# A planner in the kernel fixes the order of TensorE, VectorE and ScalarE

## The chip, the cores and the metric

The kernel runs on one core of a Trainium2 chip. Its engines are TensorE (PE in the profile, with PEld for its weight loads), VectorE (DVE), ScalarE (ACT), GpSimd (POOL, which also issues DMAs here) and SyncE (SP, which only issues DMAs). Each takes its own queue of instructions in order, and waits for the others by semaphores. The metric is the device time of one execution, in microseconds (us); lower is better.

## What is computed

Two layers on x of shape 4 x 1024 x 256, all in float32. Each has a mixer `s` and a gate `g` on the normalized x, and adds `s * silu(g)`. The parts that matter, cut from the reference:

```python
x = L0_attn_x
xn = _layernorm(x)
s = _L0_attn_ref(xn, ...)            # linear attention on cos/sin features, then an MLP
g = _silu(_L0_ffn_ref(xn, ...))      # r * (relu(k)**2 @ W_v), tokens mixed with the one before
x = x + s * g
xn = _layernorm(x)
s = _L1_attn_ref(xn, ...)            # Mamba: convolution, then the scan below
g = _silu(_L1_ffn_ref(xn, ...))      # two of eight experts for each token, one after the other
x = x + s * g

# _L1_attn_ref: token after token, 512 channels x 16 states
dA = exp(dt_t[:, :, None] * A)
h = h * dA + (dt_t * u_t)[:, :, None] * B_t[:, None, :]
y = einsum('bcs,bs->bc', h, C_t)
```

## The kernel before

**Tiling.** Tokens are cut into 8 blocks of 512. Layer 0 works on two blocks (`s`) of each of 4 sequences (`b`). `before_attention` normalizes a block (`normalize`, L195 to L214: statistics L202 and L203 on DVE, a power on POOL at L205 and L212, the product at L218), transposes it and makes queries, keys and values (the bias of the values is added at L273). `cycle` (L1190) takes one group of features at a time: `project_keys` or `project_queries` (matmuls fk at L425, fq at L436), `fractions` (L458 to L461: the rounding on ACT at L460 or DVE at L458, the fraction on DVE at L461), `sines` on ACT, and `use_keys` or `use_queries` (kv at L497, pa at L528). `after_attention` does the rest of layer 0 for a block: output projection po (x at L306), MLP ph and py (x at L350), gate g (L388), and writes the block to DRAM; the router's logits `gate` come at L411.

**Scans.** In layer 1 a block's 512 channels are two units of 256, and each unit has 16 scan steps, one for each state: 8 x 2 x 16 = 256 steps. For a step `decay` (L636) loads B and C (`bcs`, L642, by SP, three buffers) and makes `da` on ACT (L192, four buffers); `scan_step` (L690) multiplies on DVE (L710), scans (L713 or L719), and multiplies by C (L728); PE transposes and adds into `y` (L731). `prepare_block` (L549) makes `u` for a block: its load `xt` (L553), matmul pi, the convolution on DVE (L572), SiLU, and matmul pd. `prepare_unit` makes `dt` (L610 to L616) and `dtu` (L628). At the end of a unit `ys` (L756) multiplies by the gate, and `project_block` copies the projection `s` (L781) and stores it in `branch`.

**Experts.** `experts` (L844) ranks the tokens on DVE (L889 to L958), giving `slot` (L945); POOL scatters all tokens into `slots` in 32 indirect DMAs (L968). Then 23 tiles of 256 tokens run twice: `fetch` (weights `we` L982, rows `xs` L987), `hidden_layer` (pxs L1001, xst L1005, ph and ht L1017), `output_layer` (po, es L1030, xs L1034 and L1039) and two scatters. The last normalization is at L1085 to L1105.

**What sets the order.** The Python code calls these parts as generators: `Stream.step` takes the next piece of a stream, and `cycle` deals out pieces of the four streams (attention before, attention after, scan side work, experts) between two scan steps. That is only the order in which instructions are written down. The framework's own scheduler then orders each engine's instructions by this priority, by data and by buffers, with a cost model of its own; it also puts in the semaphores. One chain was fixed by hand: `in_turn` (L171) ties each special function of ACT, and each load of an activation table, to the one before, so that tables are not loaded back and forth:

```python
def in_turn(i):
    if last[0] is not None:
        tc.add_manual_dep(i.ins, last[0].ins.name, ...)   # NoSync: order alone
    last[0] = i
```

Of the kernel before, what the change touches and what calls it, by code (L numbers as in the profile page):

```python
# [2 lines left out]

# [15 lines left out]
PSUM = bass.MemoryType.PSUM  # L19
DRAM = bass.MemoryType.DRAM  # L20

P = 128
# [33 lines left out]
for _n, _w in _COLS:  # L56
    COL[_n] = NCOL
    NCOL += _w


@with_exitstack
def kernel(
# [3 lines left out]
    nc = tc.nc  # L66
# [22 lines left out]
    def tokens(ap):  # L89
        return ap.rearrange("(t p) d -> p t d", p=P)  # L90
# [75 lines left out]

    now, last = [None], [None]

    def in_turn(i):  # L171
        if last[0] is not None:
            tc.add_manual_dep(
                i.ins, last[0].ins.name,
                mybir.DependencyInfo(
                    mybir.DependencyClass.NoSync, mybir.DependencyReason.SCHED_ONLY
                ),
            )
        last[0] = i

    def functions(which):
        if now[0] != which:
            in_turn(
                nc.scalar.preload_act_table_set(  # L184
                    {"E": "natural_log_exp_and_others", "S": "silu_and_others"}[which]
                )
            )
            now[0] = which

    def special(out, in_, func, **kw):  # L190
        functions("E" if func in (AF.Exp, AF.Ln) else "S")
        in_turn(nc.scalar.activation(out, in_, func, **kw))  # L192
# [278 lines left out]
    turns = [0]  # L471
# [8 lines left out]
    kv, kvp, pa, at = {}, {}, {}, {}  # L480
# [207 lines left out]
    sums, late = {}, []  # L688
# [76 lines left out]
    def branch_halves(j):  # L765

        for i in range(NT // 2):
            ps = bank(f"ps_{j}{i}").rearrange("p (u d) -> p u d", u=2)
            for w in range(2):
                sl = slice((2 * i + w) * P, (2 * i + w + 1) * P)  # L770
                accumulate(
                    ps[:, w, :],
                    [(halves[j, c // UNIT][:, c % UNIT, sl], wout_s[:, c, :]) for c in range(NDI)],
                )
            yield ps
# [30 lines left out]
    ready, projected, left = [], set(), []  # L806
# [20 lines left out]
    for k, t in enumerate(slots):  # L827
        a = t[:NPAD, :].rearrange("(a p) d -> p a d", p=P)
# [281 lines left out]
    def finish(j, xm, s, xn):  # L1110

        for i, ps in enumerate(branch_halves(j)):
            two = slice(2 * i, 2 * i + 2)
            nc.vector.tensor_tensor(s[:, two, :], ps, xn[:, two, :], ALU.mult)
            nc.vector.tensor_tensor(s[:, two, :], s[:, two, :], xm[:, two, :], ALU.add)
            first = j * TB + 2 * i * P
            nc.sync.dma_start(out=tokens(out[first : first + 2 * P, :]), in_=s[:, two, :])
# [142 lines left out]
    turn_half(NBLK - 1, 1)  # L1260
    for one in left:
        finish(*one)


def _layout(inputs):
# [68 lines left out]
```

## Time and profile before

| | us |
|---|---|
| three runs | 2339.23, 2330.81, 2336.70 (median 2336.7) |
| the profiled execution | 2339.8 |
| its span, first to last instruction | 2338.1 |

The profile is of one execution. Its first part gives the busy time of each engine, its second the same in 40 slices of 58 us. The costliest groups, with line, engine, operation, tiles and shapes, count, busy us, mean ns, and the idle time before them with what ended it:

| group | count | busy us | mean ns |
|---|---|---|---|
| L192 ACT `da`, 128x512 | 512 | 334.4 | 716 |
| L731 PE `y`, 128x128 | 2048 | 314.1 | 302 |
| L728 DVE `da`, 128x1024 | 256 | 310.8 | 1215 |
| L713 DVE scan, 128x1024 | 128 | 290.7 | 2281 |
| L710 DVE `h`, 128x1024 | 240 | 288.6 | 1212 |
| L719 DVE scan, 128x512 | 224 | 276.2 | 1267 |
| L184 ACT table load | 134 | 171.9 | 1283 |

The run has stages: until about 300 us only layer 0 works; until about 1450 us layer 0 and scans lie beside each other; then the ranking and the scatters, and from about 1540 us experts and scans to the end. A wait is listed with the instruction that waited, what released it, the total in us, how often, and the longest.

### The profile page before, as it was taken

How to read it: one execution, taken by the hardware profiler on the slowest of the kernel's cores; microseconds unless marked ns; L12 is line 12 of the kernel's file. 1: busy time of each engine (PE TensorE's matmuls, PEld its weight loads, DVE VectorE, ACT ScalarE, POOL GpSimd, SP SyncE). 2: the span in 40 equal slices, each digit the busy share in tenths (PEclk: the TensorE clock that was granted, in tenths of full speed). 3: DMA queues.
4: the chain of work that ended last, by engine and by line, in shares of the span. 5: the costliest groups of instructions: out<-in, count | busy, mean ns of one | idle time of the engine just before them, and what ended most of it. 6: DMA issues, size and time to landing. Idle time of an engine off the chain costs nothing. (4 is left out here: it accounts for less than half of the span.)

```text
span 2338.1 us, 25455 instructions
## 1 busy us (share of the span) xinstructions
PE 1866.2 (80%) x9192; PEld 1263.9 (54%) x9192; DVE 1938.3 (83%) x2508; ACT 1388.2 (59%) x2039; POOL 499.7 (21%) x459
## 2 busy tenths in 40 slices
PE   7898688889888979879896866278988779898755
PEld 3434355444655535545464644166777567767644
DVE  5554499997899898798898889759879887978898
ACT  4654378887687877886865353235443545453674
POOL 1001000011010110100011020755435334443210
PEclk8799689789989989988898787589999899999876
DMA  9601133322333323233244454667777656766543
GB/s 275 163 9 46 45 114 94 106 67 74 86 86 104 101 60 105 83 85 105 82 105 112 118 170 108 152 201 221 221 210 234 202 194 203 253 214 221 166 166 117
DMA packets 145086, 320.22 MB, mean 137 GB/s; under 512 B 23344, under 2 KB 43952, under 8 KB 139072
## 3 DMA queue, kind: packets, MB, share of 16 engines
q1 hardware_dynamic: 110704, 170.02, 28.0%
q0 software_dynamic: 34256, 148.58, 18.5%
q8 instruction: 72, 1.18, 0.2%
q14 instruction: 54, 0.44, 0.1%
HBM read 256.86 MB, written 61.69 MB: 136 GB/s over the span
## 5 line engine op out<-in xcount | busy, mean ns | idle before, releaser
L192 ACT ACTIVATE da<-dt,neg_a 128x512 f32<-128x512 f32 x512 | 334.4, 716 | 119.3 <-PE y L731 74.5
L731 PE MATMUL y<-ident,da 128*128 128x128 f32 x2048 | 314.1, 302 | 102.7 <-DVE da L728 98.0
L731 PEld LDWEIGHTS y<-ident,da 128*128 128x128 f32 x2048 | 262.4, 156 | 184.5 <-issue 78.5
L728 DVE TENSOR_TENSOR da<-h,bcs 128x1024 f32<-128x1024 f32 x256 | 310.8, 1215 | 1.9
L710 DVE TENSOR_TENSOR h<-dtu,bcs 128x1024 f32<-128x1024 f32 x240 | 288.6, 1212 | 28.5 <-DMA bcs<-bcd 27.4
L713 DVE TENSOR_TENSOR_SCAN h<-da,h 128x1024 f32<-128x1024 f32 x128 | 290.7, 2281 | 23.2 <-ACT da L192 22.8
L719 DVE TENSOR_TENSOR_SCAN h<-da,h_tail,h 128x512 f32<-128x512 f32 x224 | 276.2, 1267 | 24.7 <-ACT da L192 24.5
L100 PE MATMUL ph<-xst,we 128*128 128x256 f32 x736 | 186.5, 411 | 34.0 <-ACT xst L1005 32.7
L100 PEld LDWEIGHTS ph<-xst,we 128*128 128x128 f32 x736 | 147.9, 206 | 64.4 <-ACT xst L1005 43.1
L184 ACT ACT_TABLE_LOAD x134 | 171.9, 1283 | 3.1 <-PEq L1319 0.8
L100 PE MATMUL po<-we,ht 128*128 128x256 f32 x736 | 168.0, 381 | 1.0 <-ACT ht L1017 1.0
L1017 ACT ACTIVATE ht<-ph,we 128x256 f32<-128x256 f32 x184 | 79.5, 470 | 123.9 <-PE ph L100 123.1
L100 PEld LDWEIGHTS po<-we,ht 128*128 128x128 f32 x736 | 136.3, 190 | 27.9 <-ACT ht L1017 5.4
L100 PE MATMUL ph_b<-x3t_b,w_b 128*128 128x512 f32 x256 | 127.0, 643 | 11.7 <-DVE fs_q L461 5.1
L100 PE MATMUL py_b<-w_b,ht_b 128*128 128x256 f32 x512 | 118.3, 390 | 4.0 <-DVE fs_q L461 4.0
L100 PEld LDWEIGHTS py_b<-w_b,ht_b 128*128 128x128 f32 x512 | 99.2, 196 | 24.3 <-DVE fs_q L461 5.1
L1005 ACT COPY xst<-pxs 128x512 f32<-128x512 f32 x46 | 26.9, 585 | 133.8 <-PE pxs L1001 133.8
L461 DVE SCALAR_TENSOR_TENSOR fs_k<-fs_k,fk 128x512 f32<-128x512 f32 x128 | 81.0, 677 | 28.7 <-ACT fs_k L460 28.6
L436 PE MATMUL fq<-qt_a,bd 32*128 32x512 f32 x256 | 94.7, 732 | 10.1 <-DVE fs_q L461 3.1
L460 ACT ACTIVATE fs_q<-fq,round_c 128x512 f32<-128x512 f32 x112 | 69.9, 689 | 53.4 <-PE fq L436 36.6
L528 PE MATMUL pa<-fs_q,kvp 128*32 128x512 f32 x512 | 93.6, 668 | 7.8 <-ACT fs_q L192 7.7
L460 ACT ACTIVATE fs_k<-fk,round_c 128x512 f32<-128x512 f32 x108 | 67.4, 690 | 53.6 <-PE fk L425 49.1
(239 smaller groups left out, 3510.9 us busy)
## 6 DMA issues: line engine op xcount, KB each, us to landing
bcs<-bcd SPq DMA_DIRECT2D x240, 512.0 KB, 5.2
xs<-slots POOLq DMA_DIRECT2D x23, 516.0 KB, 4.2
x<-in_x_dram POOLq DMA_DIRECT2D x23, 512.0 KB, 5.0
slots<-blank SPq DMA_DIRECT2D x1, 11776.0 KB, 48.8
w_b<-in_w_dram POOLq DMA_DIRECT2D x16, 512.0 KB, 4.3
w_b<-in_w_dram POOLq DMA_DIRECT2D x32, 256.0 KB, 3.3
xs<-slots POOLq DMA_DIRECT2D x23, 260.0 KB, 4.5
slots<-blank SPq DMA_DIRECT2D x1, 5888.0 KB, 30.6
```

Of the source, the lines that this page charges most:

```text
L100: nc.tensor.matmul(ps, lhs, rhs, start=i == 0, stop=i == len(pairs) - 1)
L184: nc.scalar.preload_act_table_set({"E": "natural_log_exp_and_others", "S": "silu_and_others"}[which])
L192: in_turn(nc.scalar.activation(out, in_, func, **kw))
L436: nc.tensor.matmul(ps[r], bd_s[rows, par, :], qt[rows, m, :], start=True, stop=True)
L460: nc.scalar.activation(t[:, 0, :], ps[r], AF.Identity, bias=round_c)
L461: nc.vector.scalar_tensor_tensor(t[:, 1, :], t[:, 0, :], -ROUND, ps[r], ALU.add, ALU.subtract)
L528: nc.tensor.matmul(pa[b, s][32 * r : 32 * r + 32, :], kvp[b][:, e, 4 * m + r, par, :], features(fs, r)[:, e, :], start=(par, e) == (0, 0), ...
L710: nc.vector.tensor_tensor(h, dtu, bcs[:, 0:1, :].to_broadcast([P, UNIT, TB]), ALU.mult)
L713: nc.vector.tensor_tensor_scan(flat, da.rearrange("p w t -> p (w t)"), flat, 0.0, ALU.mult, ALU.add)
L719: nc.vector.tensor_tensor_scan(h[:, w, :], da[:, w, :], b[w], h_tail[:, c, n : n + 1], ALU.mult, ALU.add,)
L728: nc.vector.tensor_tensor(da, h, bcs[:, 1:2, :].to_broadcast([P, UNIT, TB]), ALU.mult)
L731: nc.tensor.matmul(y[:, t, w * P : (w + 1) * P], da[:, w, t * P : (t + 1) * P], ident, is_transpose=True, start=False, stop=(n, t % 2, w) ...
```

## The change

A new function `arrange` is called once, after all instructions are written down and before the framework schedules them. It reads the list of instructions and works out:

- **what must come before what**: by overlapping reads and writes of each tile or DRAM tensor; by the chain of special functions (`special_order`, kept by `in_turn`); and by pools (instructions on tiles of layer 0's pools before those that first touch the experts' pools, which take their place).
- **how long each takes**: weights in ns by kind, shape and engine, and for a DMA its bytes on one queue at 260 bytes/ns with 2000 ns until it has landed.
- **an order**: it plays the list through in time. On each engine, when it is free, the ready instruction that was written down first is taken, if its tiles have a free buffer (`room`); a matmul of 32 rows or columns holds one of four strips of the array.

At the end each instruction of TensorE, VectorE and ScalarE is tied to the one before it on its engine by an order-only dependency. The orders that it found for POOL and SP are not tied; the framework's scheduler still sets those, and places all semaphores. No instruction of the computation is added or removed.

```diff
+SIGNAL, LANDING, PER_BYTE = 60.0, 2000.0, 1 / 260
+ENGINES = ("PE", "DVE", "Activation")
...
+        if kind == "InstMatmult":
+            n = _elements(outs[0])
+            self.weight = 0.84 * (max(n, P) if i.is_transpose else 2 * n)
...
+        if self.dma:
+            self.weight = 60.0
+            if engine == "Pool":
+                self.weight = 1300.0 if any(o.dynamic_ap_info is not None for o in outs + ins) else 740.0
+            self.bytes = 4
...
+        if engine == "Activation":
+            w = 165 + 0.84 * n + 75 * min(scalars, 1)
+        elif engine == "Pool":
+            w = 1250.0 if kind == "InstTensorTensor" else 200 + 0.8 * n
+        elif engine == "DVE":
+            w = 143 + 1.053 * n
...
+                if i.is_tensor_tensor_scan:
+                    w = 150 + 2.08 * n + 60 * (scalars > 0)
+                elif i.is_scalar_tensor_tensor:
+                    w += 60 * (scalars > 0)
+                else:
+                    psum = any(o.bass_ap.tensor.space == PSUM for o in ins[:1])
+                    w = 160 + (1.053 if psum else 0.516) * n + 60 * scalars
...
+        self.weight, self.hidden = w, 90.0 if w > 190 else 0.0
...
+def arrange(tc, nc, turns, early_pools, late_pools):
...
+    for k in late:
+        for of in early.values():
+            nodes[k].before |= of
+    for a, b in zip(turns, turns[1:]):
+        nodes[names[b]].before.add(names[a])
+    for k, x in enumerate(nodes):
+        x.before.discard(k)
+        for m in x.before:
+            nodes[m].after.append(k)
+        x.left = len(x.before)
...
+    def room(k):
+        new = nodes[k].uses - held
+        for name in new:
+            of = tags[tag_of[name]]
+            if of.free == 0 or of.tiles[of.at] != name:
+                of.parked.append(k)
+                return False
+        for name in new:
+            of = tags[tag_of[name]]
+            of.free, of.at = of.free - 1, of.at + 1
+            held.add(name)
+            again(tag_of[name])
+        return True
...
+        while touched:
+            engine = min(touched)
+            touched.discard(engine)
+            while ready.get(engine) and free.get(engine, 0.0) <= now:
+                k = heapq.heappop(ready[engine])
+                if not room(k):
+                    continue
+                x = nodes[k]
+                order.setdefault(engine, []).append(x.i)
+                if x.strips:
+                    start = max([now] + [strips[s] for s in x.strips])
+                    for s in x.strips:
+                        strips[s] = start + x.weight
+                    free[engine] = start + (7 if len(x.strips) == 1 else x.weight)
+                    end = start + x.weight + 150
+                elif x.dma:
+                    free[engine] = now + x.weight
+                    queue = max(queue, free[engine] + 300) + x.bytes * PER_BYTE
+                    end = queue + LANDING - 300
+                else:
+                    end = now + x.weight
+                    free[engine] = end - x.hidden
+                heapq.heappush(events, (free[engine], k, "free"))
+                heapq.heappush(events, (end + SIGNAL, k, "end"))
+                for m in x.after:
+                    follows = nodes[m].engine == engine and not x.dma and k not in nodes[m].data
+                    heapq.heappush(events, (free[engine] if follows else end + SIGNAL, m, "wait"))
+    for engine in ENGINES:
+        for a, b in zip(order[engine], order[engine][1:]):
+            tc.add_manual_dep(
+                b, a.name,
+                mybir.DependencyInfo(
+                    mybir.DependencyClass.NoSync, mybir.DependencyReason.SCHED_ONLY
+                ),
+            )
...
-    now, last = [None], [None]
+    now, last, special_order = [None], [None], []
...
+        special_order.append(i.ins.name)
...
+    arrange(tc, nc, special_order, ("w0", "keep0", "work0"), ("routes1", "moe1"))
```

## The prediction

> **What bounds the kernel now.** I read the busy shares first, then the slices of time, then the waits of the busiest engine, stage by stage.
>
> ```profile
> PE 1866.2 (80%) x9192; PEld 1263.9 (54%) x9192; DVE 1938.3 (83%) x2508; ACT 1388.2 (59%) x2039; POOL 499.7 (21%) x459
> ...
> PE   7898688889888979879896866278988779898755
> ...
> DVE  5554499997899898798898889759879887978898
> ...
> PEclk8799689789989989988898787589999899999876
> ```
>
> DVE (VectorE) is busy for 1938.3 of 2338.1 us, so it idles for 399.8. No instruction is added or removed by the change, so 1938 us is a floor; only idle time can go. The table by stage (core, then us and count for PE, PEld, DVE, ACT, POOL, then clock, DMA share, GB/s) says where it lies:
>
> ```profile
> 0.00:300.00 300.00, 239.85 (x1097) 119.55 (x1098) 154.35 (x335) 153.08 (x225) 31.45 (x55) 0.82 0.41 109
> 300.00:1500.00 1200.00, 976.57 (x4852) 613.67 (x4851) 1079.30 (x1389) 832.73 (x1108) 144.82 (x176) 0.86 0.36 99
> 1500.00:1600.00 100.00, 62.06 (x326) 53.34 (x327) 64.43 (x66) 32.20 (x57) 56.19 (x38) 0.79 0.68 211
> 1600.00:2338.00 738.00, 587.67 (x2920) 477.31 (x2918) 640.26 (x721) 370.16 (x650) 267.26 (x191) 0.88 0.64 200
> ```
>
> DVE idles 146 us in the first stage (attention alone, no scans yet), 121 in the second (attention and scans), 36 at the start of the experts, 98 afterwards (experts and scans). The DVE's own waits (us in total, times, longest) over the run:
>
> ```profile
> DVE es L1030 <- PE po L100: 49.5, 5, 34.2
> ...
> DVE h L710 <- DMA bcs<-bcd: 27.4, 22, 3.9
> DVE h L719 <- ACT da L192: 24.5, 7, 10.9
> DVE h L713 <- ACT da L192: 22.8, 9, 12.5
> ...
> DVE dt L610 <- ACT ln L192: 17.0, 6, 5.5
> ...
> DVE st_a L202 <- DMA x<-in_x_dram: 8.3, 1, 8.3
> ...
> DVE x_b L218 <- POOL rs_b L205: 7.5, 8, 1.1
> ```
>
> The reader is to see many short waits for other engines and few long ones: an engine takes its queue in order, so a result that is 2 us late costs 2 us even where ready work stands behind it. This is what an order can mend.
>
> **What the change does to the order.** I compared the two built programs, engine by engine. The instructions are the same, 134 table loads (171.9 us) included. On DVE some 375 of 2508 stand in their old place (median shift 5 places), on PE 2266 of 5990 (median 3), on ACT 1162 of 2039 (median 0); SP keeps 268 of 318 and POOL 387 of 456, shifted by 4 and 8 places at most. So the change is real but local. No wait between engines is new in kind: the chain is of one engine with itself. Built wait instructions go from 548 to 463 on DVE and from 366 to 434 on ACT; the gaps of DVE under 0.3 us sum to only some 14 us, so I cost this at nothing.
>
> To price a shift I take a DVE instruction that waits, follow its releaser back to the DVE instruction that began the chain, and sum the DVE durations that stand between the two in each built order (rows of the trace, less 0.08 us each, the overlap of neighbours). If that distance grows by d, the wait shrinks by up to d; if it shrinks, the wait grows.
>
> Start. In the old order the statistics of the second tile of x stand before the work of the first and wait 8.3 us for their load; in the new one 20 instructions (12.6 us) go first. But these were ready only later: PE gives fk at 26 to 29 us. What is late next is that PE, freed about 2 to 3 us sooner because v_a L273 no longer stands behind the second tile: **-3 us**. The other 135 us of this stage I leave: PE is 80% busy, and its first 600 instructions move by 2 places on average. x L350 waits 28.3 us for matmuls in both orders (distances 4.3 to 4.3 and 6.9 to 6.3).
>
> 300 to 1500. Distances, old to new: the POOL power function (rs, 19.0 us of waits in this stage, a round trip of 1.1 us) 0 to 2.3, 0 to 1.7, 0 to 5.8; dt L610 behind ln (12.4 us) 12.8 to 22.0 and 8.1 to 17.7; fs L461 behind ACT (21.7 us) 8.8 to 18.1; h behind da (9.7 us) 8.7 to 16.2; h L710 behind the bcs load (13.2 us) 3.5 to 27.5 and 4.0 to 16.6, but also 2.3 to 2.3. By this rule 76 of the 117 us of waits over 0.3 us would go. That is the upper end: it takes every chain to last as before, and elsewhere distances shrink (fs at 466 us by 15, g_b at 1384 by 11, ys at 745 by 10), which costs nothing only if PE delivers sooner too. The lower end is what was ready in the gap by the trace and is now put into it: 9 us. I take half of the upper, **-38**, because side work moves ahead on PE and DVE alike. Against it, u L572 waits for PE pi; its distances shrink from 17.4 to 5.8 (at 1366 us) and from 9.2 to 1.1 (at 1834): **+20** for the two, behind an xt load that SP cannot issue earlier.
>
> Start of the experts. es L1030 waits 34.2 us because POOL's 32 scatters only begin at 1466 us, when DVE has worked out the slots. In the old order slot L945 stands behind scan step 135 and the first es behind step 143, 45.7 us of DVE work apart; in the new order behind steps 130 and 142, 62.2 apart. The scatters last the same. **-16.5**. What hides it is scan work that used to stand in front; if ACT starves those scans, the wait returns as h <- da.
>
> 1600 to the end. h behind da (37.5 us): 36.5 to 42.5, 41.8 to 46.0, 19.2 to 28.6; bcs loads 12.9 us, mostly covered. Upper end 36 of 90, lower end 10; half: **-18**. The ACT waits for the branch stores (s L781, 43.8 us) keep their place, hence not more.
>
> Sum: -3 -38 +20 -16.5 -18 = -55.5. Against the profiled run (2339.8 us; span 2338.1) that is 2284; the runs' median, 2336.7, is 3 lower, so I say **2283 us**.
>
> **Two rules that speak against it.** The new planner prices a 512-wide f32 matmul at 0.84 x 2 x 512 = 860 ns, 430 a pass. The trace has 3.60 us for 8 passes of pbk_a (450 each) but 5.10 for the 8 of pbq_a just before, and 6.52 for the 8 of pd at 284 us, after 14 us without a matmul: 815 each. [...] For the eight block preparations pd comes 3.1 us later than planned: up to 25 us if DVE stood behind each, none if scans cover it. I count it within the +20.
>
> For loads the planner has 2.0 us plus bytes at 260 GB/s, one queue: 4.0 us for bcs. The row says 5.2 us (median). [...] Above 1600 us DMA is 64% busy[...]. By the row the buffers of xs (three) stand ahead by two tiles, and es waits only 15.3 us in all there. I side with the row.
>
> **Rivals.**
> - The waits go in full, since PE idles too (449 us of gaps, 75 of them filled by ready matmuls in the new order): -3 -76 +20 -16.5 -36 = -112, 2228 us. For it: nearly all distances widen in 300 to 1200. Against it: shrinking ones lie beside them.
> - Off to the same: each wait removed uncovers one of like size, since DVE is already 90% busy in 300 to 1500; only the expert start remains, less the 20 at u: about 2336.
> - Slower: the order is too early for the experts. es stands about 9 us of DVE work (5 to 15) earlier beside the scans than before; distances to it go from 33.9 to 23.3, 25.6 to 15.2, 11.8 to 3.6. If PE and the gathers don't come sooner, DVE stands still about 8 us in each of the six scan units there (48) and 20 at u, while only the waits filled by ready work go (about 27): +41, 2381 us. It decides if po reaches es more than 5 us late in most units. For it: indirect DMAs last 1.7 to 1.9 us on POOL, where the plan has 1.3. Against it: POOL is only 36% busy after 1600.
> - That the chain does nothing is excluded by the built order.
>
> **How the numbers follow.** Forecast 0.55, full gain 0.14, off to the same 0.13, slower 0.18. From no change I can tell 0.5% (12 us). The forecast and the full gain are faster; of the third case a fifth falls on that side, and of the slower case a tenth is too small to tell: faster 0.72, same 0.11, slower 0.17. Range 2230 (full gain) to 2345 (nothing gained, a little lost); the slower case is left out. The likeliest alone spans 2250 to 2320.
>
> **What would show it.** DVE busy still about 1938, idle near 345. The wait of es at the expert start 15 to 20 us; waits for POOL rs and for bcs in 300 to 1500 under half. u L572 behind pi grown at two block preparations. I am wrong if es L1030 waits more than 30 us after its first tile, if h behind da grows, or if the second stage has DVE idle above 110 us.

## The result and the profile after

The changed kernel takes 2307.98 us (median of 4 runs, 2302.16 to 2314.62) beside 2336.01 us for the kernel before on the same chip (4 runs): a ratio of 0.9883, 95% interval 0.9844 to 0.9922. Run again unaltered in two later batches it gave 0.9838 (0.9807 to 0.9868) and 0.9859 (0.9826 to 0.9893). It is faster, by 1.2 to 1.6%; 2283 had been forecast, with a range of 2230 to 2345. The profiled execution took 2302.16 us, with a span of 2300.4. (Lines stand 246 or 247 further down in the changed kernel: es L1030 is L1277 there, da L728 is L975; in e_attn and e_exp they stand 2 lines lower still, in e_late and e_late_scat 4.)

The busy shares and slices of the changed kernel:

```profile
PE 1883.4 (82%) x9192; PEld 1269.7 (55%) x9192; DVE 1941.6 (84%) x2508; ACT 1395.5 (61%) x2039; POOL 495.2 (22%) x459
...
DVE  4563569899988999889899899959979988997998
...
PEclk8789689789988989979898787589999899999866
```

DVE does the same work (1941.6 us for 1938.3) and idles 358.8 us instead of 399.8. Where the 41 went is read from the table by stage. I cut it at 330 and 1480 us, not at 300 and 1500 as before: one wait of 14 us (fs_k behind ACT) ends at 297 us in the old kernel and at 305 in the new one, so a cut at 300 would book it in different stages, and the wait at the start of the experts would be cut in two as well. Columns: stretch, its length, DVE busy (instructions), granted TensorE clock, DMA share, GB/s. Before:

```profile
0.00:330.00 330.00, 184.35 (x364) 0.82 0.40 108
330.00:1480.00 1150.00, 1029.40 (x1343) 0.87 0.36 98
1480.00:1600.00 120.00, 84.32 (x83) 0.74 0.68 199
1600.00:2340.00 740.00, 640.26 (x721) 0.88 0.64 199
```

After:

```profile
0.00:330.00 330.00, 175.97 (x354) 0.81 0.39 105
330.00:1480.00 1150.00, 1047.88 (x1358) 0.86 0.36 102
1480.00:1600.00 120.00, 93.89 (x101) 0.84 0.69 206
1600.00:2340.00 740.00, 623.90 (x697) 0.89 0.61 194
```

Length less busy time is the idle time (in the last row up to the end of the span): 145.7 to 154.0 in the first stage (+8.3), 120.6 to 102.1 in the second (-18.5), 35.7 to 26.1 at the start of the experts (-9.6), 97.8 to 76.5 afterwards (-21.3). That is -41.1, and with 3.3 us more of busy time -37.8, which is the difference of the spans (2338.1 to 2300.4) but for rounding. In two more executions of the change (a_again and a_third in the table of the experiments) the first row is 7 us higher and the other three lie within 4 us of these.

Over the whole run the waits of DVE over 0.3 us fall behind ACT from 131.1 to 90.0 us, behind DMA from 43.1 to 13.4 and behind POOL from 33.2 to 13.9, and rise behind PE from 180.9 to 230.9. The gaps below 0.3 us hardly change (11.5 to 10.6 us), so that there are fewer wait instructions on DVE is not what made the gain.

**Second stage.** The waits of DVE from 330 to 1480 us (total, times, longest), before:

```profile
DVE h L710 <- DMA bcs<-bcd: 13.2, 12, 3.3
DVE fs_k L461 <- ACT fs_k L460: 12.9, 7, 5.0
DVE dt L610 <- ACT ln L192: 12.4, 4, 5.5
DVE fs_q L461 <- ACT fs_q L460: 8.8, 6, 6.0
DVE h L719 <- ACT da L192: 7.8, 3, 3.9
DVE gate L411 <- PE pgt_b L100: 6.9, 5, 2.0
...
DVE x L218 <- POOL rs_cb L205: 5.6, 7, 0.9
```

After:

```profile
DVE fs_q L708 <- ACT fs_q L707: 22.2, 24, 2.9
DVE gate L658 <- PE pgt_b L346: 20.6, 7, 4.5
DVE fs_k L708 <- ACT fs_k L707: 14.7, 13, 3.1
...
DVE h L957 <- DMA bcs<-bcd: 2.8, 1, 2.8
...
DVE x_b L465 <- POOL rs_b L452: 1.8, 2, 0.9
...
DVE h L960 <- ACT da L439: 0.5, 1, 0.5
```

The reader is to see an exchange. The waits for bcs (13.2 to 2.8), for ln (12.4 to 6.3), for da (9.7 to 0.5, in two rows before) and for POOL's power function (19.0 to 1.8, in four rows before) are gone or halved: 43 us less. In their place attention and gate work stands at the head of DVE's queue before its partner is done: fs behind ACT 21.7 to 36.9, in 37 waits instead of 13, and gate behind PE 6.9 to 20.6. These two alone give back 29 us. PE in turn stands longer in front of the scans' results, the row of the kernel before first, then that of the changed one (330 to 1480 us):

```profile
PE y L731 <- DVE da L728: 47.6, 21, 6.7
```

```profile
PE y L978 <- DVE da L975: 83.6, 28, 7.9
```

On balance the attention runs further ahead of the scans. The last router gate ends at 1381.1 us, before at 1405.3, and slot at 1436.5, before at 1465.1, while scan step 128 is hardly earlier (1412.4, before 1414.4).

**Experts.** The waits from 1600 us on, before:

```profile
DVE h L713 <- ACT da L192: 20.8, 7, 12.5
DVE h L719 <- ACT da L192: 16.7, 4, 10.9
DVE es L1030 <- PE po L100: 15.3, 4, 8.8
DVE h L710 <- DMA bcs<-bcd: 12.9, 9, 3.9
```

After:

```profile
DVE es L1277 <- PE po L346: 47.0, 17, 12.8
DVE h L957 <- DMA bcs<-bcd: 5.4, 4, 1.8
```

Again an exchange (da 37.5 to almost nothing, es 15.3 to 47.0), but with a profit. The lead of 28.6 us at slot is 22.6 at the first es, 34 at the last es of the first pass and 39 at that of the second, and scan step 256 ends 39.5 us sooner.

### The profile page after: what moved, and what is told of

The parts are those of the page before. It is cut to its first block, busy times and chain, and to the rows that moved or that the text cites. A ratio compares the mean times of both kernels' runs of the same rounds, so it can differ in the third digit from the quotient of the medians.

```text
span 2300.4 us, 25432 instructions
## 1 busy us (share of the span) xinstructions
PE 1883.4 (82%) x9192; PEld 1269.7 (55%) x9192; DVE 1941.6 (84%) x2508; ACT 1395.5 (61%) x2039; POOL 495.2 (22%) x459
## 5 line engine op out<-in xcount | busy, mean ns | idle before, releaser
L978 PE MATMUL y<-ident,da 128*128 128x128 f32 x2048 | 328.1, 308 | 152.6 <-DVE da L975 135.3
L978 PEld LDWEIGHTS y<-ident,da 128*128 128x128 f32 x2048 | 268.4, 158 | 254.4 <-DVE da L975 127.8
L975 DVE TENSOR_TENSOR da<-h,bcs 128x1024 f32<-128x1024 f32 x256 | 312.0, 1219 | 0.6
L960 DVE TENSOR_TENSOR_SCAN h<-da,h 128x1024 f32<-128x1024 f32 x128 | 291.2, 2284 | 2.1 <-ACT da L439 0.5
L966 DVE TENSOR_TENSOR_SCAN h<-da,h_tail,h 128x512 f32<-128x512 f32 x224 | 278.8, 1273 | 0.6
L346 PE MATMUL ph<-xst,we 128*128 128x256 f32 x736 | 181.3, 402 | 34.9 <-ACT xst L1252 34.6
L346 PE MATMUL ph_b<-x3t_b,w_b 128*128 128x512 f32 x256 | 121.6, 618 | 4.0 <-ACT dt L851 2.1
L775 PE MATMUL pa<-fs_q,kvp 128*32 128x512 f32 x512 | 106.3, 702 | 12.5 <-ACT fs_q L439 12.4
L708 DVE SCALAR_TENSOR_TENSOR fs_q<-fs_q,fq 128x512 f32<-128x512 f32 x128 | 82.3, 683 | 24.9 <-ACT fs_q L707 24.3
L744 PE MATMUL kv<-fs_k,v_a 128*32 128x256 f32 x1024 | 83.7, 465 | 23.0 <-ACT fs_k L439 22.9
```

Source lines behind the costliest of these rows:

```text
L346: nc.tensor.matmul(ps, lhs, rhs, start=i == 0, stop=i == len(pairs) - 1)
L708: nc.vector.scalar_tensor_tensor(t[:, 1, :], t[:, 0, :], -ROUND, ps[r], ALU.add, ALU.subtract)
L744: nc.tensor.matmul(kv[b][r // 2][32 * g : 32 * g + 32, r % 2, :, :], v[:, t, h * DH : (h + 2) * DH], f[:, :, m, par, :], start=(s, t, r % ...
L775: nc.tensor.matmul(pa[b, s][32 * r : 32 * r + 32, :], kvp[b][:, e, 4 * m + r, par, :], features(fs, r)[:, e, :], start=(par, e) == (0, 0), ...
L960: nc.vector.tensor_tensor_scan(flat, da.rearrange("p w t -> p (w t)"), flat, 0.0, ALU.mult, ALU.add)
L966: nc.vector.tensor_tensor_scan(h[:, w, :], da[:, w, :], b[w], h_tail[:, c, n : n + 1], ALU.mult, ALU.add,)
```

## The experiments

Each kernel was timed beside the kernel before on the same chip, in three batches (medians of the kernel before: 2343.99, 2343.62 and 2340.93 us): e_attn, e_exp, e_pe98 and e_scat in the first; a_again, e_only_dve, e_only_pe and e_sig in the second; a_third, e_late, e_scat_again and e_late_scat in the third. In the first batch the unaltered change was not among them. Where the expectations use letters: E puts the gain down to the new order of the expert stage by itself, H to the head start that the attention stage gives the experts; D says that the order of DVE alone does it, W that the orders of the three engines are only good together; L says that the plan expects results sooner than they come, so that slack in it would help; P and S put such waits down to a price that is too low, P of the matmuls, S of the scatters. I give DVE's idle time in the four stages of the table above for every run, since that is where causes show (us, one profiled execution each):

| kernel | to 330 | 330-1480 | 1480-1600 | 1600-end | span | ratio, 95% interval |
|---|---|---|---|---|---|---|
| before | 145.7 | 120.6 | 35.7 | 97.8 | 2338.1 | 1 |
| change | 154.0 | 102.1 | 26.1 | 76.5 | 2300.4 | 0.9883 [0.9844, 0.9922] |
| a_again | 161.4 | 103.3 | 29.6 | 79.4 | 2315.5 | 0.9838 [0.9807, 0.9868] |
| a_third | 161.3 | 103.2 | 26.5 | 74.7 | 2307.7 | 0.9859 [0.9826, 0.9893] |
| e_attn | 154.3 | 96.5 | 40.0 | 104.0 | 2334.6 | 0.9952 [0.993, 0.9974] |
| e_exp | 145.3 | 135.1 | 28.0 | 80.8 | 2328.8 | 0.9929 [0.9907, 0.9951] |
| e_pe98 | 153.0 | 90.5 | 30.0 | 88.1 | 2305.1 | 0.9853 [0.9817, 0.9889] |
| e_scat | 154.1 | 101.5 | 23.0 | 73.9 | 2295.8 | 0.9813 [0.9781, 0.9844] |
| e_scat_again | 154.0 | 102.8 | 23.1 | 66.8 | 2290.4 | 0.9794 [0.9765, 0.9823] |
| e_late | 149.4 | 103.4 | 28.0 | 77.0 | 2298.3 | 0.9822 [0.9787, 0.9856] |
| e_late_scat | 148.7 | 103.4 | 23.3 | 74.4 | 2292.3 | 0.9837 [0.9801, 0.9873] |
| e_sig | 163.8 | 100.0 | 42.4 | 90.3 | 2331.7 | 0.994 [0.9916, 0.9963] |
| e_only_dve | 156.8 | 134.5 | 33.2 | 116.7 | 2380.4 | 1.0106 [1.0074, 1.0138] |
| e_only_pe | 154.1 | 155.5 | 26.0 | 111.9 | 2393.6 | 1.0176 [1.0142, 1.021] |

### Half of the change at a time

The program is split where its text begins with the experts' part (`l0.close()`); e_attn chains only what is written ahead of it, e_exp only what is written behind.

```diff
+    split = nc.cur_bb.bb.instructions[-1].name
     l0.close()
...
+    at_split = max(k for n, k in names.items() if n == split or k == 0)
     for engine in ENGINES:
-        for a, b in zip(order[engine], order[engine][1:]):
+        mine = [i for i in order[engine] if (names[i.name] <= at_split)]
+        for a, b in zip(mine, mine[1:]):
```

(e_exp has `>` in place of `<=`.)

> Only the instructions written down before the experts (layer 0, and the scans beside it) are chained in the planner's order; those of the expert part, with the scans written there, keep the framework's order. The kernel before takes 2336, the change 2308. Theory E (the gain is made in the expert part; the attention part is neutral): 2328 to 2338. Rival H (head start: in the change the last router logits come 24 us earlier, 1381 for 1405 us, because side work runs ahead of the scans, and that alone lets the experts start sooner): 2310 to 2320, and the first es about 20 us earlier than 1543. If the attention part were a loss of its own, as the first stage suggests (router logits of block 0 at 259 for 251 us): above 2340.

> The other half: only the expert part is chained, layer 0 keeps the framework's order. Theory E: 2300 to 2312, with the first stages as before (first logits at 251 us) and the es wait at the expert start below 25 us. Rival H: 2322 to 2332, since the last logits come at 1405 us again and the first es with them. If both halves are needed and add up, the two gains sum to 28 us.

Measured: 2333.08 and 2328.38 us beside 2343.99, so 11 and 16 us of gain; the two ratios multiply to 0.9881, which is what the whole change gives within the intervals. Neither half carries it alone: e_attn lies where E expected it and e_exp where H did, so each theory missed on the other half. In e_attn slot ends at 1441.9 us and the first es at 1521.7, the head start of the whole change (22 us). Then it melts: by the last es of the first pass 9.9 us are left of it, at scan step 256 3.3. The waits of e_attn say why:

```profile
DVE es L1279 <- PE po L348: 49.2, 6, 32.5
...
DVE h L959 <- DMA bcs<-bcd: 26.8, 20, 3.6
DVE h L962 <- ACT da L441: 24.3, 9, 12.9
```

Over the run these are the waits of the old expert stage, nearly as long as in the kernel before (es 49.5, bcs 27.4, da 47.3 there, 39.7 here with 15.4 at L968). In e_exp it is the other way round: the first es ends where it did before (1544.0), and its expert stage has the low idle time of the change (28.0 and 80.8). The rows of the table fit together: the first two stages of e_attn and the last two of e_exp sum to 154.3 + 96.5 + 28.0 + 80.8 = 359.6 us, and the whole change has 358.7. So each half makes its gain in its own stage. Each also loses elsewhere when it is alone (e_attn 10.5 us behind 1480, e_exp 14.5 from 330 to 1480). Of e_exp's 14.5 us, 11.4 lie between 1400 and 1480 (DVE busy for 65.0 us there, 76.4 before), where the two halves meet; what is late there was not followed further.

### One engine alone

```diff
-ENGINES = ("PE", "DVE", "Activation")
+ENGINES = ("DVE",)
```

> Only VectorE's order is chained; TensorE, ScalarE, POOL and SP are ordered by the framework around it. Theory D (the bound engine's order carries the gain): 0.984 to 0.993. Rival W (a VectorE order is good only with the TensorE order that it was planned with; else es, fs and gate wait more): 1.000 or slower, with VectorE's waits for PE up by 30 us or more.

> Only TensorE's order is chained. Theory D: 0.997 to 1.003, since VectorE falls back to the framework's order. Rival W: a gain of its own, 0.992 to 0.997, because side work's matmuls come sooner.

Measured: 2371.19 and 2388.72 us, 1.1% and 1.8% slower than the kernel before. Two of the longest waits of each, e_only_dve first, where one of the waits for ln lasts 31.3 us:

```profile
DVE es L1277 <- PE po L346: 55.2, 19, 9.0
DVE dt L857 <- ACT ln L439: 53.1, 11, 31.3
```

```profile
DVE h L957 <- DMA bcs<-bcd: 40.9, 32, 3.2
DVE h L966 <- ACT da L439: 37.6, 18, 5.2
```

The 31.3 us lie at the expert start. The rows of ACT there, in e_only_dve (start, duration, then the idle time before it):

```profile
1530.99 0.59 ACT L1252 COPY xst<-pxs 128x512 f32<-128x512 f32 x1 [29.83 <-PE pxs L1248]
1531.48 1.06 ACT L439 ACTIVATE ln<-dtu 128x1024 f32<-128x1024 f32 x1
```

In the framework's order ACT has the first expert tile (xst) ahead of ln and stands 29.8 us for it; in the planned order DVE wants ln ahead of es, so it stands too. In the change ACT has this ln done at 1468 us, ahead of xst. An order of PE alone leaves DVE's scans waiting for bcs and da. D falls on both kernels. W holds for DVE alone, whose waits for PE rise from 181 to 254 us, but it had given PE alone a small gain (0.992 to 0.997), which did not come. ACT alone, and two engines of three, were not run.

### The prices in the plan

Three edits change only what the plan believes, and so the order:

```diff
-SIGNAL, LANDING, PER_BYTE = 60.0, 2000.0, 1 / 260
+SIGNAL, LANDING, PER_BYTE = 400.0, 2000.0, 1 / 260
```

```diff
-            self.weight = 0.84 * (max(n, P) if i.is_transpose else 2 * n)
+            self.weight = 0.98 * (max(n, P) if i.is_transpose else 2 * n)
```

```diff
-                self.weight = 1300.0 if any(o.dynamic_ap_info is not None for o in outs + ins) else 740.0
+                self.weight = 2000.0 if any(o.dynamic_ap_info is not None for o in outs + ins) else 740.0
```

> The planner's time for a signal from one engine to another is 400 ns for 60, so it leaves slack before each reader on another engine; all three engines chained. Theory L (the waits for fs and gate that came with the change are many short ones, 0.8 us each for fs_q, which a third of a us of slack mends): fs and gate waits in sum 80 us in the change, here under 55, and 0.978 to 0.984. Rival: slack in the plan only moves the same work about, since VectorE has nothing else ready then: 0.984 to 0.993.

> The planner's matmul weight is 0.98 for 0.84 (0.84 over the mean granted clock of 0.861); all else as in the change. Theory P (new DVE waits for fs, gate and py_b, 51, 21 and 10 us in the second stage, come from a plan in which TensorE is too fast): those three fall by a third or more in sum, 2290 to 2300. Rival: they hang on the chain of activations and on the clock's two states, which a mean doesn't mend: 2302 to 2316, the three sums within 15 us of the change's.

> The planner's weight of an indirect DMA on POOL is 2000 ns for 1300 (the scatters at the expert start come every 1.8 us in the trace). Theory S (DVE stands 24.6 us at the first es because the plan has the 32 scatters end some 16 us too soon): the wait falls below 8 us, 2288 to 2298. Rival: what was placed ahead of it is missing later, or DVE waits for da instead, since ACT has buffers for two scan steps only: 2302 to 2314 though the es wait shrinks.

**e_sig**, 0.34 us of slack on nearly every dependence: 2333.09 us, a ratio of 0.994 where the unaltered change has 0.9838 in the same batch, so some three fifths of the gain are lost. The waits for fs and gate, which L expected below 55 us, are 72.4 over the run (80.4 in the change). The second stage stays good (100.0), but the start (163.8) and the expert start (42.4) are worse: the first es ends at 1547 us, 26 us later than with the change. The edit does more than its expectation says: `arrange` charges SIGNAL also where an instruction of DVE or ACT uses what the same engine wrote just before, as a scan does. So slack of this kind loses time, but slack between engines alone was not run, and L is refuted only in this form.

**e_pe98**, dearer matmuls: 2309.51 us, no different from the change. Its waits were exchanged once more:

```profile
DVE x L597 <- PE py_b L346: 36.3, 5, 16.6
DVE h L960 <- ACT da L439: 32.4, 9, 10.2
...
DVE es L1277 <- PE po L346: 15.4, 7, 6.3
```

es (71.6 in the change) went down to 15.4, and da came back (53.5 with the 21.1 at L966; 0.5 in the change at L960). The table shows it by stage: 12 us better in the second, 16 worse in the experts' two. The waits that P was about (fs, gate and py_b from 300 to 1480 us) fell from 81 to 64 us, less than the third that P asked for and a little more than the rival's 15; in time the rival's range holds. The clock's two states, which it names, are the 0.50 and 1.00 of the rows in the last section; that the waits hang on them was not shown.

**e_scat**, dearer indirect DMAs (the 32 scatters, and with them the loads of `we` and the scatters of each tile): 2301.60 us. Its order is that of the change up to the expert part. POOL's rows show what the price is for. In the kernel before, the 32 scatters begin at 1466.03 us and the first load of xs behind them is issued at 1525.98 (start, duration, then the idle time before it):

```profile
1466.03 1.43 POOL L968 DMA_INDIRECT slots<-rows,slot  x1 [7.54 <-DVE owner L957]
...
1525.98 0.78 POOL L987 DMA_DIRECT2D xs<-slots  x1 [0.61 <-DMA slots<-rows,slot]
```

In the changed kernel:

```profile
1437.85 1.42 POOL L1215 DMA_INDIRECT slots<-rows,slot  x1 [4.14 <-DVE wrow L1208]
...
1504.39 0.77 POOL L1234 DMA_DIRECT2D xs<-slots  x1 [4.73 <-DMA slots<-rows,slot]
```

That is 60.0 us before and 66.5 after; the scatters themselves take 57.9 and 60.5, one every 1.8 to 1.9 us, where the plan has 1.3 (41.6 for 32). So the plan expects es some 20 us too early. The waits for es from 1480 to 1600 us, in the change and in e_scat:

```profile
DVE es L1277 <- PE po L346: 24.6, 1, 24.6
```

```profile
DVE es L1277 <- PE po L346: 6.0, 2, 5.5
```

With the price of 2000 ns, scan work stands in front of it: scan step 144 ends at 1504.6 us (change 1533.3), the first es waits 5.5 us, although it ends later (1530.3, change 1521.4). The wait fell as S had it; the time lies between S's range and that of its rival, whose waits for da did come (15.6 us over the run, 0.5 in the change).

### Start and expert start, in one batch

e_late begins the chains behind the first scan step, so that the first stage keeps the framework's order; what follows it is ordered as in the change. e_late_scat has both edits.

```diff
     strips, queue = [0.0] * 4, 0.0
+    cut = {}
...
+                if not cut and getattr(x.i, "is_tensor_tensor_scan", False):
+                    cut.update({e: len(order.get(e, [])) for e in ENGINES})
                 order.setdefault(engine, []).append(x.i)
...
-        for a, b in zip(order[engine], order[engine][1:]):
+        mine = order[engine][cut[engine]:]
+        for a, b in zip(mine, mine[1:]):
```

> The changed kernel itself, unaltered, beside the next three on one chip: by every theory 0.985 to 0.992 of the kernel before.

> The changed kernel once more, unaltered, so that the three kernels beside it can be set against it on one chip: 0.984 to 0.989 of before, about 2308 us. All theories expect the same.

> The chains begin only behind the first scan step; what the plan places ahead of it stays in the framework's order, what follows has the order of the change. If the first stage really loses 8 us by the new order (the second tile's statistics on VectorE then end at 37.7 us where they ended at 21.6), the first router logits come back from 259 to about 251 us and most of that reaches the end: 2300 to 2303 us, 0.98 to 0.983. If the 8 us are the scatter of the profiled executions, or if they are made good later by waits that open in their place, 2306 to 2310 us.

> Indirect DMAs priced at 2000 ns by the plan where the change has 1300, as run before at 2301.6 us. If the wait of es at the expert start (24.6 us with the change, 5.5 us with this price) is worth what the earlier run suggests, it lies 5 to 8 us below the changed kernel on the same chip. If the earlier difference was chance, the two lie within 3 us.

> Both edits in one kernel. If the two losses lie at different places and are independent, the gains add up: 10 to 15 us below the changed kernel, about 2295 us, 0.977 to 0.98 of before. If time won early is only turned into a longer wait at the expert start or behind it, it lies no lower than the better of the two alone, about 2301 us.

**a_again and a_third**, the change unaltered: 2308.14 and 2309.92 us. Their profiled executions are 15 and 7 us longer than the first one of the change, and 7 us of that lie in the first stage, with the same order: by the first router gate they are 8.7 us behind (267.4 and 267.6, against 258.8). The cause is in the granted clock (0.59 from 120 to 140 us in both, 0.84 in the first profile of the change), see the last section.

**e_late**: 2298.58 us. The first router gate ends at 250.0 us, as before the change (250.8). In all four executions with the framework's order of this stage it ends between 249.6 and 250.8, and in those with the change's order between 257.6 and 259.3 or, in a_again and a_third, at 267.4 and 267.6; so the new order loses about 8 us there. Of these 2.7 are lost by 150 us, and 4.2 more from there to the first x behind py_b, where the granted clock is lower (0.83 for 1.00 from 150 to 180 us). The rows of PE from 150 to 180 us (busy, instructions, granted clock, DMA share, GB/s), before, then the change (e_late has 1.00 there too, with 107 matmuls done):

```profile
150.00:180.00 30.00, 27.56 (x113) 1.00 0.05 18
```

```profile
150.00:180.00 30.00, 25.51 (x84) 0.83 0.03 9
```

In the change PE first stands 3.9 us for x_b (1.5 before); then the eight matmuls of pbq_a take 5.63 us where they took 3.67, and the first x behind py_b ends at 183.4 us instead of 176.5. How much of the 8 us reaches the end is open. The median lies 11 us below a_third's, as if all of it did, but the intervals of the ratios (0.9822 and 0.9859) overlap. Against the change's first profile e_late is 5 us ahead at scan step 128 and 2 us at step 256, since the es waits come out as long (70.0 in all).

**e_scat_again**: 2293.05 us against 2309.92 for the change on the same chip, and the two intervals do not touch; the difference is larger than the 5 to 8 us expected. The waits concerned:

```profile
DVE es L1277 <- PE po L346: 46.0, 24, 5.5
...
DVE h L960 <- ACT da L439: 15.8, 3, 10.0
```

es falls from 71.6 to 46.0 and da takes back 15. Of the 17.3 us between the spans of this batch 7.5 lie in front of scan step 128, where the orders are the same and the clocks are not (from 120 to 140 us 0.82 beside a_third's 0.59), so I put them down to the clock; about 10 are left for the edit (4.6 in the earlier pair of e_scat and the first profile of the change). It has the lowest ratio of this study, in two batches: 0.9813 and 0.9794 of before.

**e_late_scat**: 2297.62 us, about that of e_late and no lower than the better of the two edits alone. The gains do not add up; at the expert start it has e_scat's short wait, and 7.6 us more idle time behind 1600 us than e_scat_again.

## Why the prediction was right, and by how much it was off

The direction and the kind of gain were right: no work removed, idle time of DVE down from 399.8 to 358.8 us (about 345 had been said), nothing from the chain as such. The size was not: the sum had -55.5 us, the two profiles differ by 37.7 and the medians of the three pairs by 28 to 35, half to two thirds. Term by term, from the profiles:

- **Start, -3: measured +8.3.** The wait for the load of x went (8.3 us), as said; DVE now waits 12.1 us there for the first tile's pv_a. PE was freed 2 to 3 us sooner, as said (DVE's first fk step ends at 28.0 us instead of 30.2). The step that failed is the next one, "The other 135 us of this stage I leave". The statistics of the second tile, put behind the first tile's work, end at 37.7 us instead of 21.6, and that tile's v_a then ends 1.9 us late (72.2 for 70.3). About half of the loss, 4.2 us, comes with the granted clock from 150 to 180 us, 0.83 for 1.00 (e_late). The prediction looked for slow matmuls at the block preparations (pd, 815 ns each); they cost time here, pbq_a 5.63 us for 3.67.
- **Second stage, -38 and +20: measured -18.5.** The net is right by luck, since neither term is. The distance rule held for the waits it was worked out on: POOL, bcs, ln and da lost 43 us. It cannot see waits that did not exist, and fs, gate and py_b grew by 33. Other waits, v_a and g_b among them, gave the rest. "I take half of the upper" was a fair allowance in kind and 20 us short in size. And the +20 for u behind pi did not come: all waits of u over the run are 11.3 us, before 12.3. The reason given for it, "an xt load that SP cannot issue earlier", did not hold: SP issues that load at 1335 us where it was 1354, and at 1788 where it was 1822, and PE's waits for xt fall from 13.6 to 0.6 us over the run. So the slow matmuls counted under that term (pd, 815 ns each where 430 was planned) cost DVE nothing visible at u, and e_pe98, which charges PE more, gains nothing in the sum.
- **Expert start, -16.5: measured -9.6.** The term "the scatters last the same" was mis-sized: from the first scatter to the first xs load takes 6.5 us longer, 2.6 in the scatters and 4.1 in a wait for their landing. 16.5 less 6.5 is 10.0, against 34.2 - 24.6 = 9.6 measured. The profiles hint at why the landing takes longer. In ten of the fourteen profiled executions SP issues a 512 KB load of bcs within 4.2 us of the last scatter's end, and the first xs load follows that end by 3.3 to 6.0 us; in the other four (before, e_attn, e_sig, e_only_dve) there is no such load and it follows by 2.0 to 2.3. The scan work that fills the gap brings these loads with it. No run tests this.
- **1600 to the end, -18: measured -21.3.** Right in size, in part by luck: the da and bcs waits went further than the upper end of 36 (50.4 to 5.4), and es took back 32. Longer waits at es had been put only into the rival "slower", which is not what happened, because the experts' work did come sooner. For loads the trace's row (5.2 us for bcs, where the plan has 4.0) was the right guide: the waits for bcs fell from 12.9 to 5.4 us and PE's waits for xs in this stage rose only from 15.1 to 18.3, so no large loss by loads that land behind the plan was shown.

Of the sizes named as signs, the idle time came near (358.8 us for 345) and the wait at the expert start did not (24.6 us, not 15 to 20). Of the signs that I had named for being wrong, two appeared: es waits 47.0 us after its first tile, and DVE idles 113 us between 300 and 1500 us (102 between 330 and 1480; the rest is mostly the one long wait that moved across the border). They meant lost gains, not a loss. The rival "off to the same" describes the mechanism of the second stage better than the forecast did, yet not its net. Three sums in the prediction are slightly off, without weight for the outcome: 55.5 us below the median of 2336.7 is 2281, not 2283; "off to the same" comes to 2340, not 2336; and its shares give 0.12 for the same and 0.16 for slower.

What stays open: why each half alone loses in the other stage, whether the bcs loads are what delays the scatters' landing, how much of the first stage's loss reaches the end, and whether the dearer matmuls of e_pe98 for the attention and the price of e_scat for the experts could be had together; that kernel was not run.

## What to carry to other kernels

In a stage where DVE was 90% busy, a wait that the new order removed was mostly replaced by one that had been hidden: book such terms by what is left after the exchange, here 18 of 43 us. An order from one plan should be imposed on all engines that the plan moved: on DVE or PE alone it made this kernel 1 to 2% slower. And look first at the plan's price of a long chain that everything waits for (32 scatters, one every 1.8 to 1.9 us, not 1.3): of the three prices changed here it was the only one that helped, while slack on every edge, or dearer matmuls everywhere, moved the waits. When a new order moves where TensorE stands still, look at the granted clock behind it too: here PE stood 3.9 us for x_b where it had stood 1.5, the clock from 150 to 180 us was 0.83 for 1.00, and about half of the loss in the first stage came with it. That the longer stand lowered the clock was not shown.

## What the hardware showed that was not expected

The same order can run its first stage 8.7 us apart, by the granted clock. The PE rows from 120 to 150 us (busy, instructions, granted clock, DMA share, GB/s), first profile of the change, then a_third:

```profile
120.00:150.00 30.00, 28.89 (x107) 0.89 0.00 1
```

```profile
120.00:150.00 30.00, 29.20 (x69) 0.56 0.00 0
```

PE is busy throughout in both, and gets 107 matmuls done at 0.89 and 69 at 0.56. A matmul of fq (32 x 512) takes 1056 or 1217 ns at the low clock (0.50) and 587 or 692 at the high one (1.00). The orders are the same and at 120 us the two lie less than 1 us apart. A finer cut of a_third shows the clock go up and come back:

```profile
120.00:131.50 11.50, 11.50 (x37) 0.50 0.00 0
131.60:134.90 3.30, 2.53 (x10) 1.00 0.00 0
135.00:150.00 15.00, 15.00 (x26) 0.50 0.00 1
```

In the change's first profile it goes up at 126.5 us and stays at 1.00 to 150 us. In a_third PE is busy for all of 135 to 150 us and stays at 0.50. Why the clock did so, no run here shows. Over whole executions the time goes with it: in 32 runs of the kernel before on one chip the mean clock lay between 0.852 and 0.868 and the time between 2332 and 2359 us, with a correlation of -0.77 and 1.6 us per 0.001 of clock. Two profiles can thus differ by 8.7 us in a stage that no edit touched, and a comparison of landmarks has to begin behind it.

An indirect scatter on POOL takes between 0.96 and 3.04 us of issue for the same shape (the 32 of each of the two profiles), in no order that I could find.
